# From coroutine stages with hand-set due times to one list schedule over single instructions, in a two-layer transformer kernel

## The chip, the cores and the metric

The kernel runs on one core of one Trainium2 chip. The metric is the device time of one execution in microseconds (us). A core has five engines, each with its own in-order instruction stream: PE (the matrix engine; its weight loads are listed apart as PEld), DVE (vector), ACT (scalar, which evaluates functions), POOL and SP (which here only issues DMAs). PE writes only to PSUM, which DVE and ACT read; the rest of the data lies in SBUF.

## The reference

2048 tokens of width 128 (four sequences of 512, here called blocks 0 to 3) pass through four residual sublayers. In short:

```
x = x + attention(layernorm(x))    # causal, 16 heads of 8
x = x + moe(layernorm(x))          # 8 experts of width 512, gelu, top 2,
                                   # a capacity per expert counted over all tokens in order
x = x + gated_recurrence_and_ffn(layernorm(x))
    # q, k, v, gate: 128 -> 1024; state = decay*state + k*v along the sequence;
    # out = gate*q*state -> Wo; then layernorm, 128 -> 512 -> 128 with gelu
x = x + ternary_ffn(layernorm(x))  # silu(x W1)*(x W2), two 512 -> 512 layers with gelu, 512 -> 128
```

The blocks are independent of each other but for one thing: the running count of tokens per expert goes from block to block in the routing.

## The kernel before, in words

Each block goes through eight stages: **project** (layernorm, transposes, q and k for groups of four heads, v), **maxima** (a first pass over the scores for the row maxima: PE writes `s`, DVE reduces it to `mx`), **weights** (scores again less the maxima, ACT takes `exp` into `ex`, POOL cuts the triangle, PE multiplies by v into the one PSUM bank `po`), **output** with **route** (layernorm, logits, a string of small DVE operations, then 8 indirect DMAs that put each token into rows of `xgd`), **experts** (read the rows back as `xg`, two layers for each of 8 experts, results to `ygd`, 8 indirect DMAs `got` back), **recurrence** (8 chunks of 128 channels: four projections `pp`, a scan on DVE, then `por`), **feed** (the gelu layer) and **ternary** (four layers, each operand split into a high and a low part `hh`, `hl`). A ninth stage, **setup**, loads constants and writes the rounded ternary weights (`round_weights`, lines 975 to 989: DMA to `stage`, POOL rounds and subtracts, DVE reduces to `odd`, which tells whether the general path at the end of the kernel is needed; it is not taken with these inputs).

PSUM holds three single banks that all dense work shares (`bank()`, tag `pt`), two pairs of banks for scores (`s`) and one for `po`. Expert weights `ew` have three buffers, recurrence weights `rw` three.

PE, DVE, ACT and SP run their instructions in the order in which the program issues them. That order is made while the kernel is built. Every stage is a Python coroutine that issues a piece and yields. `play` (line 305) picks the next piece: it keeps a modelled clock of each engine (`Clock`, line 50, with the cost of each operation in `cost`, line 123), looks at which stages could go on at PE's present time, and takes the one whose due time `start` is lowest; the due time then grows by the PE work of the piece times a `stretch`. Start and stretch are set by hand per stage (lines 1096 to 1105), at 140 us a block:

```python
    at = 140.0 * b
    stages[f"project{b}"] = Stage(-4e3, 1.0, "pt", project(b))
    stages[f"maxima{b}"] = Stage(max(at - 145.0, 0.0), 3.5, "s", maxima(b))
    stages[f"weights{b}"] = Stage(-5e3 if b else 1.0, 1.0, "s", weights(b))
    stages[f"experts{b}"] = Stage(at, 1.3, "pt", experts(b))
    stages[f"recurrence{b}"] = Stage(at + 60.0, 1.0, "pt", recurrence(b))
    stages[f"feed{b}"] = Stage(at + 158.0, 1.4, "pt", chain(feed(b), ternary(b)))
```

A stage also yields names of other stages that it waits for. Some are data dependences. Others are order alone: `weights{b}` waits for `experts{b-1}` and `feed{b-2}` (lines 442 to 448), `experts{b}` for `experts{b-1}`, `recurrence{b}` for `recurrence{b-1}`, `feed{b}` for `output{b+1}` and `feed{b-1}`. Within a piece the instructions stand as the stage writes them, and each operation has one engine, written in the code: for instance the copies of transposes on ACT, the copy of `po` on DVE, the triangle on POOL.

Of the kernel before, what the change touches and what calls it, by code (L numbers as in the profile page):

```python
# [10 lines left out]
F32 = mybir.dt.float32  # L11
# [9 lines left out]
P = 128  # L21
D = 128
# [21 lines left out]
def block_kernel(ctx: ExitStack, tc: tile.TileContext, i: dict, out: bass.AP):  # L44
# [4 lines left out]

    class Clock:  # L50

        def __init__(self):
            self.now = dict.fromkeys(("PE", "DVE", "ACT", "POOL", "SP"), 0.0)
            self.used = {}
            self.turns = {}
            self.end = self.work = 0.0
            self.table = None

        def span(self, ap):
            if ap.tensor.name not in self.used:
                self.used[ap.tensor.name] = []
                tag = getattr(ap.tensor, "tag", None)
                if tag is not None:
                    self.turns.setdefault(tag, []).append(ap.tensor)
            if ap.space == DRAM:
                lo = ap.offset
                hi = lo + sum(s * (n - 1) for s, n in ap.ap)
            else:  # L70
                lo = ap.offset % ap.ap[0][0]
                hi = lo + sum(s * (n - 1) for s, n in ap.ap[1:])
            return lo, hi

        def bufs(self, tensor):
            return tensor.bufs or tensor.tag_meta.bufs

        def over(self, tensor):
            return max((x[4] for x in self.used.get(tensor.name, ())), default=0.0)

        def slot(self, tag):

            t = self.turns.get(tag, ())
            return self.over(t[-self.bufs(t[-1])]) if t and len(t) >= self.bufs(t[-1]) else 0.0

        def ready(self, engine, ap, write):
            lo, hi = self.span(ap)
            at = 0.0
            for x in self.used[ap.tensor.name]:
                if x[3] != engine and x[0] <= hi and lo <= x[1] and (write or x[2]):  # L90
                    at = max(at, x[4])
            tag = getattr(ap.tensor, "tag", None)
            if tag is not None and not self.used[ap.tensor.name]:
                t = self.turns[tag]
                n = self.bufs(ap.tensor)
                if len(t) > n:
                    at = max(at, self.over(t[-1 - n]))
            return at

        def note(self, engine, op, args, kw):  # L100
            out = kw["out"] if "out" in kw else args[0]
            ins = [x for x in (*args, *kw.values()) if isinstance(x, bass.AP) and x is not out]
            ins += [x.ap for x in (*args, *kw.values()) if isinstance(x, bass.IndirectOffsetOnAxis)]
            took, after = self.cost(engine, op, out, ins, kw, args)

            who = "PUT" if op.startswith("indirect") and out.space == DRAM else "DMA" if "dma" in op else engine
            at = max([self.ready(who if who == "PUT" else engine, out, True)] + [self.ready(engine, x, False) for x in ins])
            begin = max(self.now[engine], at)
            self.now[engine] = begin + took
            end = begin + took + after  # L110
            for x, write in [(out, True)] + [(x, False) for x in ins]:
                lo, hi = self.span(x)
                keep = self.used[x.tensor.name]
                if write:
                    keep[:] = [k for k in keep if not (lo <= k[0] and k[1] <= hi)]
                keep.append((lo, hi, write, who, end))
                if len(keep) > 64:
                    keep[:] = [k for k in keep if k[4] > self.now["PE"] - 300.0]
            self.end = max(self.end, end)
            if engine == "PE":  # L120
                self.work += took

        def cost(self, engine, op, out, ins, kw, args):
            n = out.free_size()
            if "dma" in op:
                size = 4.0 * math.prod(out.shape) if engine != "POOL" else 4.0 * P * P
                return {"SP": 0.45, "ACT": 0.1, "POOL": 1.0}[engine], 1.9 + size / 2.0e5
            if engine == "PE":
                if op == "transpose":
                    return 0.11, 0.2  # L130
                w, x = kw["lhsT"], kw["rhs"]
                n = x.free_size()
                if w.partition_size() == HP:
                    return max(0.03, n * 1.7e-4), 0.2
                if w.free_size() < HP and n > HP and w.free_size() == DK + 1:
                    return max(0.11, n * 6.5e-4), 0.2
                if w.dtype == F32:
                    return max(0.22, n * 1.68e-3), 0.2
                return max(0.06, n * 4.5e-4), 0.2
            if engine == "ACT":  # L140
                load = 0.0
                f = args[2] if op == "activation" else None
                if f in (AF.Exp, AF.Gelu) and f != self.table:
                    self.table, load = f, 1.3
                return load + (0.22 + 9.1e-4 * n if n <= S else 0.42 + 4.9e-4 * n), 0.1
            if engine == "DVE":
                if op == "tensor_reduce":
                    n = ins[0].free_size()
                    return 0.06 + 1.08e-3 * n, 0.1
                if op == "tensor_tensor_scan":  # L150
                    return 1.25, 0.1
                if n <= 64:
                    return 0.12, 0.1
                if op in ("tensor_copy", "memset") and all(x.space != PSUM for x in ins):
                    return 0.1 + 6.5e-4 * n, 0.1
                return 0.1 + 1.2e-3 * n, 0.1
            if op == "memset":
                return 0.1 + 9.0e-4 * n, 0.1
            return {"affine_select": 0.6, "iota": 0.6}.get(op, 0.25 + 2.1e-3 * n if n > 64 else 1.0), 0.1

    clock = Clock()

    class Engine:
# [3 lines left out]
        def __getattr__(self, op):  # L167
            def issue(*args, **kw):
                ins = getattr(self.engine, op)(*args, **kw)  # L169
                clock.note(self.name, op, args, kw)  # L170
                return ins

            return issue

    class nc:
        vector, scalar, gpsimd, sync, tensor = (
            Engine(n, e) for n, e in (
                ("DVE", tc.nc.vector), ("ACT", tc.nc.scalar), ("POOL", tc.nc.gpsimd), ("SP", tc.nc.sync),
                ("PE", tc.nc.tensor),
            )  # L180
        )
        values_load = tc.nc.values_load

# [13 lines left out]
    small = ctx.enter_context(tc.tile_pool(name="small", bufs=4))  # L197
    scr = ctx.enter_context(tc.tile_pool(name="scr", bufs=2, space=DRAM))
    work = ctx.enter_context(ExitStack())
    att = work.enter_context(tc.tile_pool(name="att", bufs=1))  # L200
    rt = work.enter_context(tc.tile_pool(name="rt", bufs=1))
    ps_s = work.enter_context(tc.tile_pool(name="ps_s", bufs=2, space=PSUM))
    ps_o = work.enter_context(tc.tile_pool(name="ps_o", bufs=1, space=PSUM))
    pools(work, "", y=1, moe=1, ew=3, rec=2, rw=3, ff=8, p_d=1)

    work.enter_context(tc.manual_schedule(engines=IN_ORDER))
    mm = nc.tensor.matmul
# [20 lines left out]
    xs = state.tile([P, NT, D], F32, name="xs")  # L228
    x_v = i["x"].rearrange("(n p) d -> p n d", p=P)
# [9 lines left out]
    def moments(src):  # L239

        st = small.tile([P, TB, 6], F32, tag="ln_st", name="ln_st")
        mv = small.tile([P, TB, 2], F32, tag="ln_mv", name="ln_mv")
        for t in range(TB):
            nc.vector.bn_stats(st[:, t, :], src[:, t, :])
        for t in range(TB):
            nc.vector.bn_aggr(mv[:, t, :], st[:, t, :])
        return mv
# [9 lines left out]
    def layernorm(src, dst):  # L257

        mv = moments(src)
        rs = small.tile([P, 2, TB], F32, tag="ln_rs", name="ln_rs")  # L260
        nc.vector.tensor_scalar(rs[:, 0, :], mv[:, :, 1], EPS, None, ALU.add)
        nc.gpsimd.tensor_tensor(rs[:, 0, :], rs[:, 0, :], mhalf[:, 0, :], ALU.pow)
        yield WAIT
        scaled(src, mv, rs[:, 0, :], dst)
        yield WAIT

    def flip(src):

        pt = bank("pt", shape=(P, TB, P))
        for t in range(TB):  # L270
            transpose(pt[:, t, :], src[:, t, :])
        return pt
# [3 lines left out]

    def y_tile(who):
        return At.y.tile([P, TB, D], F32, tag="y" + who, name="y", bufs=2 if who == "a" else 1)

    def turned(y, who, gain=None, shift=None):  # L280
# [6 lines left out]
        return yT  # L287

    GO, WAIT = 0, 1

    def run(stage):
# [908 lines left out]
```

## Time and profile before

| | us |
|---|---|
| median of 5 runs | 835.54 (834.39 to 841.73) |
| the profiled execution: its time, its span | 834.4, 832.6 |
| mean granted PE clock in it | 0.868 of full speed |
| busy PE, PEld, DVE, ACT, POOL | 677.6, 382.0, 465.3, 279.1, 182.4 |
| DMA | 46.37 MB, mean 56 GB/s |

The span runs from the first to the last instruction; the profiled execution's time is 1.8 us longer. Where the stages lie in it, by the start of the first and last instruction of each kind, in us from the span's start:

| block | `pqk` matmuls | `mx` reductions | `exp` | expert `ph` | `pp` matmuls | first `pa` of ternary to `res` |
|---|---|---|---|---|---|---|
| 0 | 9.9 to 19.2 | 21.7 to 98.1 | 52.3 to 111.3 | 169.6 to 194.1 | 234.2 to 295.3 | 361.4 to 394.3 |
| 1 | 121.8 to 131.6 | 138.1 to 193.7 | 200.5 to 238.3 | 311.3 to 352.5 | 404.0 to 479.4 | 545.6 to 578.5 |
| 2 | 257.1 to 267.1 | 298.1 to 341.1 | 395.3 to 424.9 | 495.6 to 536.7 | 588.1 to 646.4 | 701.3 to 735.6 |
| 3 | 445.2 to 461.4 | 482.3 to 525.3 | 579.5 to 609.0 | 663.4 to 692.4 | 735.4 to 767.3 | 795.2 to 826.1 |

In the views, nearly all instructions carry line 169, the helper through which all are issued, so they are told apart by tile names. An entry `ex<-s` is the instruction that writes `ex` from `s`. Matmul ends are modelled, and matmuls overlap, so a busy PE may still be slow: the granted clock has to be read with it.

### The profile page before, as it was taken

To read this page: it belongs to the slowest core of one execution; us is meant where nothing else is said; L and a number is where in the kernel's file an instruction comes from. 1 tells how busy PE (TensorE), PEld (TensorE's weight loads), DVE (VectorE), ACT (ScalarE), POOL (GpSimd) and SP (SyncE) were. 2 spreads that over 40 slices of the span, in tenths; PEclk is the share of its full clock that TensorE was granted. 3 is DMA by queue.
4 is the path that set the end of the run, shared out by engine and by line. 5 is a ranking of instruction groups with operands and counts; after the bars stand their busy time and mean duration, and the time that the engine had idled before them with its cause. 6 is when DMAs were issued, how large, how long until landed. Compare 5 with 4: busy or idle time off the path is not lost.

```text
span 832.6 us, 9464 instructions
## 1 busy us (share of the span) xinstructions
PE 677.6 (81%) x3302; PEld 382.0 (46%) x3302; DVE 465.3 (56%) x1082; ACT 279.1 (34%) x460; POOL 182.4 (22%) x249
## 2 busy tenths in 40 slices
PE   5168977896797889969995989978998597899676
PEld 2024334394343347636442447645443385544244
DVE  5256338822357777476367667374368414778263
ACT  3022332054453213413752222414642162233221
POOL 1064220302520400042320400042321403200110
PEclk9655698588799989989998889969999798999888
DMA  6521000244001123320110113320010252021000
GB/s 150 178 66 38 3 13 1 89 122 144 13 17 35 52 62 99 95 72 1 34 36 21 58 50 106 95 60 25 14 38 33 83 146 60 10 60 29 1 0 17
DMA packets 73623, 46.37 MB, mean 56 GB/s; under 512 B 9696, under 2 KB 66528, under 8 KB 73568
## 3 DMA queue, kind: packets, MB, share of 16 engines
q1 hardware_dynamic: 70944, 41.23, 17.2%
q0 software_dynamic: 2048, 4.20, 1.7%
q8 instruction: 28, 0.46, 0.2%
q10 hardware_dynamic: 576, 0.26, 0.1%
q14 instruction: 27, 0.22, 0.1%
HBM read 35.71 MB, written 9.96 MB: 55 GB/s over the span
## 4 chain that ended last, share of the span: by engine, by line
PE 52%; DVE 25%; issue 10%; ACT 4%; SPq 3%; DMA 3%; POOL 2%; ACTq 0%; DVEq 0%; POOLq 0%
PE s L169 12%; PE ph L169 9%; PE pp L169 7%; PE po L169 6%; PE py L169 4%; PE por L169 4%; DVE mx L169 4%; PE pt L169 3%; SPq L169 3%; DVE a L169 3%; PE pqk L169 2%; DVE st L169 2%; DVE oc L169 2%; DVE hl L169 2%; DVE hh L169 2%
## 5 line engine op out<-in xcount | busy, mean ns | idle before, releaser
L169 PE MATMUL pp<-yT,rw 128*128 128x512 f32 x256 | 125.0, 621 | 4.6 <-ACT g L169 1.1
L169 DVE TENSOR_REDUCE mx<-s 128x2 f32<-128x1024 f32 (+3 forms) x128 | 100.2, 819 | 26.8 <-PE s L169 25.8
L169 ACT ACTIVATE ex<-s 128x768 f32<-128x768 f32 (+1 forms) x96 | 79.8, 880 | 63.3 <-PE s L169 60.8
L169 PE MATMUL s<-ks,qs 32*128 32x128 f32 (+3 forms) x256 | 62.5, 485 | 36.6 <-DVE mx L169 35.7
L169 PEld LDWEIGHTS pp<-yT,rw 128*128 128x128 f32 x256 | 44.8, 193 | 61.1 <-issue 32.9
L169 POOL TENSOR_TENSOR ln_rs<-ln_rs,mhalf 128x4 f32<-128x4 f32 (+1 forms) x20 | 23.7, 1187 | 208.2 <-DVE ln_rs L169 207.9
L169 POOL TENSOR_SCALAR_AFFINE_SELECT ex<-ex 128x256 f32<-128x256 f32 (+1 forms) x96 | 48.8, 512 | 92.3 <-ACT ex L169 91.3
L169 PE MATMUL po<-ex,vs 128*9 128x128 f32 (+3 forms) x512 | 53.7, 506 | 9.4 <-issue 9.1
L169 PE MATMUL ph<-hh,r_h_w 128*128 128x512 f32 x128 | 53.4, 417 | 7.3 <-DVE hh L169 6.9
L169 ACT ACTIVATE hT<-ph,w_mb 128x192 f32<-128x192 f32 x128 | 45.2, 419 | 37.0 <-PE ph L169 36.5
L169 PEld LDWEIGHTS s<-ks,qs 32*128 32x128 f32 x256 | 28.2, 217 | 63.6 <-DVE mx L169 41.8
L169 DVE TENSOR_SCALAR xT<-py,w_mb 128x192 f32<-128x192 f32 x32 | 13.4, 418 | 75.8 <-PE py L169 69.4
L169 POOL DMA_INDIRECT xgd<-y,rt_at x32 | 34.5, 1077 | 96.5 <-DVE rt_at L169 87.9
L169 PE MATMUL ph<-hl,r_h_w 128*128 128x512 f32 x128 | 53.4, 417 | 2.3 <-DVE hl L169 2.3
L169 PE MATMUL ph<-xT,ew 128*128 128x192 f32 x256 | 51.9, 340 | 0.7 <-ACT hT L169 0.5
L169 DVE COPY oT<-po 128x512 f32<-128x512 f32 x16 | 11.0, 690 | 74.0 <-PE po L169 74.0
L169 PE MATMUL pqk<-yT,wide 128*128 128x512 f32 x64 | 39.8, 763 | 15.4 <-DVE wide L169 11.4
L169 PE MATMUL s<-qs,ks 32*128 32x128 f32 (+3 forms) x256 | 41.9, 429 | 7.8 <-ACT ex L169 6.7
L169 PE MATMUL py<-hT,ew 128*128 128x192 f32 x256 | 46.8, 328 | 0.0
L169 PEld LDWEIGHTS ph<-xT,ew 128*128 128x128 f32 x256 | 42.8, 197 | 3.6 <-issue 1.7
L169 POOL DMA_INDIRECT got<-ygd,rt_at x32 | 31.2, 975 | 58.6 <-ACT ex L169 47.8
L169 PEld LDWEIGHTS s<-qs,ks 32*128 32x128 f32 x256 | 21.9, 213 | 48.2 <-ACT ex L169 35.2
(187 smaller groups left out, 1098.9 us busy)
## 6 DMA issues: line engine op xcount, KB each, us to landing
ew<-in_E_dram SPq DMA_DIRECT2D x64, 256.0 KB
xg<-xgd SPq DMA_DIRECT2D x4, 768.0 KB
ygd<-og SPq DMA_DIRECT2D x16, 192.0 KB
stage<-in_h_w_dram SPq DMA_DIRECT2D x8, 256.0 KB
rw<-in_Wk_dram SPq DMA_DIRECT2D x32, 64.0 KB
rw<-in_Wv_dram SPq DMA_DIRECT2D x32, 64.0 KB
rw<-in_Wg_dram SPq DMA_DIRECT2D x32, 64.0 KB
rw<-in_Wq_dram SPq DMA_DIRECT2D x32, 64.0 KB
```

Source lines behind the costliest of these rows:

```text
L169: ins = getattr(self.engine, op)(*args, **kw)
```

## The change

The stages become plain functions that are run once, block by block, without issuing anything: each call of an engine is noted as a task with its tiles (`Plan.note`). Tasks depend on earlier tasks that wrote or read the same data. Then `Plan.order` simulates the five engines: at each step it takes the engine whose next task can begin earliest, and among its tasks that could begin within 0.1 us of that the one with the longest path of work behind it. `Plan.issue` emits the real instructions in that order. The due times, `play`, and the waits between stages are gone. Two kinds of order between blocks are kept as `plan.hold`: a recurrence after the one of the block before, from its transposed input on, and feed with ternary after the ternary of the block before.

A tile is no longer given a buffer where the program writes it down; it gets a slot when its first task is ordered, in the order of its own stage for the small shared kinds. Some operations may go to either of two engines, whichever would end first in the model: copies out of PSUM (ACT or DVE), an expert's last bias (DVE or ACT), the high and low parts in ternary (DVE or POOL), the triangle (POOL as one instruction, or DVE as two). The model also has a PE clock of half or full speed, a price for changing ACT's function table, matmuls of 32 rows beside each other, and DMAs that land one after the other. In block 0 the maxima use single `pt` banks instead of the pairs. The layernorm tiles of recurrence, feed and ternary share one buffer (`yc`). The count of buffers and the arithmetic are otherwise as before; every matmul is there in the same number.

The core of the diff:

```diff
-    def play(live):
-        through = {}
-        while live:
...
-            now = max(clock.now["PE"], min(free.values()))
-            soon = min((t for n, t in free.items() if live[n].start < 0), default=1e9)
...
-            n = min((n for n, t in free.items() if t <= now), key=lambda n: live[n].start)
...
+        def order(self):
+            for task in reversed(self.tasks):
+                way = next(iter(task.ways.values()))
+                after = sum(way[2]) if isinstance(way[2], tuple) else way[2]
+                task.weight = way[1] + after + max((t.weight for t in task.before), default=0.0)
...
+            while len(done) < len(self.tasks):
+                best = None
+                for e in ENGINES:
+                    starts = []
+                    for task in can[e]:
+                        t = self.begin(task, e)
+                        if t is None:
+                            continue
+                        if len(task.ways) > 1:
+                            end = t + task.ways[e][1]
+                            others = [
+                                x + task.ways[o][1] for o in task.ways if o != e and (x := self.begin(task, o)) is not None
+                            ]
+                            if others and min(others) < end - 0.01:
+                                continue
+                        starts.append((t, task))
...
+                first, engine, starts = best
+                near = [(t, x) for t, x in starts if t <= first + NEAR]
...
+                t, task = max(near, key=lambda x: x[1].weight)
...
+        def begin(self, task, engine):
+            t = self.now[engine]
+            if task.table is not None and task.table != self.table:
+                t += TABLE
+            for e, r in task.ready.items():
+                if e != engine and r > t:
+                    t = r
+            for lent in task.lents:
+                if lent.slot is None:
+                    if not lent.slots.free or lent.queue[0] is not lent:
+                        return None
+                    t = max(t, min(lent.slots.until[k] for k in lent.slots.free))
+            return t
...
+    TABLE, NEAR = 1.3, 0.1
...
         if "dma" in op:
             size = 4.0 * math.prod(out.shape) if engine != "POOL" else 4.0 * P * P
-            return {"SP": 0.45, "ACT": 0.1, "POOL": 1.0}[engine], 1.9 + size / 2.0e5
+            return {"SP": 0.45, "ACT": 0.1, "POOL": 1.0}[engine], (1.6, size / 2.5e5)
...
+    def copy(dst, src):
+        with one_task():
+            nc.scalar.copy(dst, src)
+            if plan.recording:
+                nc.vector.tensor_copy(dst, src)
...
     def weights(b):
-        if b > 0:
-            yield f"experts{b - 1}"
-        if b > 1:
-            yield f"feed{b - 2}"
...
-            nc.gpsimd.affine_select(
...
+            with one_task():
+                nc.gpsimd.affine_select(
...
+                for j in range(2):
+                    nc.vector.scalar_tensor_tensor(
+                        e[:, j], e[:, j], 2.0, upper.unsqueeze(1).to_broadcast([P, len(part), P]), ALU.min, ALU.mult,
+                    )
...
     def halves(h, c):
-            nc.vector.tensor_copy(hi, h)
-            eng = nc.gpsimd if c == 1 else nc.vector
-            eng.tensor_tensor(lo, h, hi, ALU.subtract)
+            with one_task():
+                for x in (nc.vector, nc.gpsimd):
+                    x.tensor_copy(hi, h)
+            with one_task():
+                for x in (nc.vector, nc.gpsimd):
+                    x.tensor_tensor(lo, h, hi, ALU.subtract)
...
     def recurrence(b):
-        yield f"experts{b}"
-        yield f"recurrence{b - 1}" if b > 0 else "scales"
...
         if b > 0:
-            yield f"begun{b - 1}"
+            plan.hold = [lasts[b - 1]]
...
+    plan.stage = "setup"
+    setup()
     for b in range(NB):
-        at = 140.0 * b
-        stages[f"project{b}"] = Stage(-4e3, 1.0, "pt", project(b))
...
-    play(stages)
+        for stage in (project, maxima, weights, output, experts, recurrence, feed, ternary):
+            plan.stage = f"{stage.__name__}{b}"
+            stage(b)
+    plan.issue()
```

829 lines of the change are left out of this document (465 added, 364 removed).

## The prediction

> **What bounds the kernel now.** I read the page first: busy times, then the slices, then the chain.
>
> ```profile
> PE 677.6 (81%) x3302; PEld 382.0 (46%) x3302; DVE 465.3 (56%) x1082; ACT 279.1 (34%) x460; POOL 182.4 (22%) x249
> PE   5168977896797889969995989978998597899676
> PEclk9655698588799989989998889969999798999888
> PE 52%; DVE 25%; issue 10%; ACT 4%; SPq 3%; DMA 3%; POOL 2%; ACTq 0%; DVEq 0%; POOLq 0%
> ```
>
> PE is the fullest engine, and over half of the chain that ended last is PE. But a slice with a 7 or 8 for PE often has a 5 to 8 for the granted clock: PE loses time by idling, and again by being slowed. So I cut the span at the stages' borders and asked for busy time and clock in each stretch. The columns are the stretch, then busy us of PE, PEld, DVE, ACT and POOL with instruction counts, then the granted PE clock, the DMA share and GB/s.
>
> ```profile
> 0.00:45.00 45.00, 15.84 (x52) 7.38 (x52) 18.01 (x51) 6.77 (x11) 6.82 (x30) 0.79 0.56 153
> 45.00:120.00 75.00, 62.00 (x407) 28.38 (x407) 36.75 (x78) 23.11 (x29) 30.71 (x50) 0.67 0.10 29
> 120.00:169.00 49.00, 38.63 (x161) 20.13 (x162) 39.34 (x101) 6.47 (x12) 9.09 (x9) 0.65 0.14 43
> 169.00:311.00 142.00, 117.07 (x633) 65.70 (x631) 72.01 (x177) 55.81 (x96) 32.84 (x44) 0.89 0.23 65
> 311.00:496.00 185.00, 161.82 (x829) 92.39 (x830) 113.82 (x263) 70.21 (x116) 40.24 (x50) 0.93 0.18 52
> 496.00:680.00 184.00, 161.12 (x849) 98.54 (x849) 102.62 (x248) 73.96 (x131) 40.87 (x49) 0.92 0.22 65
> 680.00:735.00 55.00, 45.44 (x173) 31.03 (x172) 28.29 (x71) 17.67 (x32) 14.66 (x13) 0.91 0.15 39
> 735.00:832.60 97.60, 75.69 (x208) 38.42 (x208) 54.44 (x98) 25.11 (x37) 7.17 (x6) 0.91 0.08 23
> ```
>
> Busy PE times the clock of its stretch is roughly what the same matmuls would need at full clock: 12.5 + 41.5 + 25.1 + 104.2 + 150.5 + 148.2 + 41.4 + 68.9 = 592.3 us. The span is 832.6, so 240.3 us are lost: 155.0 idle (832.6 - 677.6) and 85.3 to the half clock (677.6 - 592.3). DVE, the next engine, has 465.3. Hence the floor for any order of these instructions is far below today's time, and the question is how much of the 240 an order can get back.
>
> The losses have places. From 311 to 680 the kernel is periodic (the chunks of recurrence 1 and 2, the expert runs and the exps of the table lie 184 us apart); there PE does (150.5 + 148.2) / 369 = 81% of full-clock work. Around it: 120 to 169 is maxima 1 and route 0 with nothing else, at 51% (25.1 / 49); 735 to the end is recurrence, feed and ternary of block 3 in series, at 71% (68.9 / 97.6); 0 to 120 is block 0's attention with setup beside it, at 45% (54.0 / 120). Three more views show typical stalls: groups of waits (us in total, times, longest), the timeline of DVE and PE, and one group of ACT.
>
> ```profile
> PE s L169 <- DVE mx L169: 36.3, 21, 19.1
> 38.16 0.17 DVE L169 TENSOR_SCALAR dec<-dec 128x8 f32<-128x8 f32 x1 [13.17 <-ACT dec L169]
> 139.35 0.69 PE L169 MATMUL s<-ks,qs 32*128 32x384 f32 x2 [4.99 <-DVE mx L169]
> L169 ACT ACT_TABLE_LOAD x8 | 10.3, 1283 | 3.3 <-issue 2.9 <-PE s L169 0.3
> 416.30:437.10 20.80, 20.67 (x142) 9.64 (x140) 12.85 (x36) 11.00 (x16) 6.04 (x10) 1.00 0.13 36
> ```
>
> The 19.1 us: PE waits for a maximum on DVE, which stands 13.17 us behind a setup instruction whose DMA comes late. The 4.99 us: DVE works through route's small operations in written order while PE waits for a reduction queued behind them. Both are order, not data. The last line, a stretch where weights, recurrence and ternary work lie beside each other, shows 99% of full-clock work: PE can be filled when three stages are open at once.
>
> **The change, step by step.** *Waits between stages go.* `weights{b}` no longer waits for `experts{b-1}` and `feed{b-2}`: attention 1 (exps from 200.5 today) can follow attention 0 (last exp 111.3) at once, and 2 and 3 behind it. Dense work of earlier blocks fills PE between the score matmuls, which today run at half clock when alone (0.67 and 0.65 above). What still binds is data: `qs`, `ks`, `vs` and `po` are single, so attentions pipeline by head group; recurrences and the feed/ternary pairs stay in series; block 3's recurrence, feed and ternary remain the end of the longest path.
>
> First 120 us: nothing but setup can lie beside block 0 there, in either order. The 19.1 us stall can go. It can also come back: the order rests on DMAs at 250 GB/s, the page's best slice moved 178, and whatever DVE has queued behind `stage` or `dec` waits as today. Bounds 0 and -19; I take -8, nearer to no gain, since the same late DMAs feed the same queue. 112 us.
>
> 120 to 735 (615 us, need 592.3 - 54.0 - 68.9 = 469.4 us, now 76%): the floor is the 99% slice, but no order holds that for 500 us, so 97% is the best end: 469.4 / 0.97 = 484. The other end is today's periodic 81%: 580. I take 88%, a little under the middle, because three shared PSUM banks stay and every evicting engine is in order: 469.4 / 0.88 = 533 us. So -82.
>
> Last 97.6 us: recurrence 3, feed 3, ternary 3 in series, need 68.9. Leftovers of block 2 may fall into it, and its own gaps may shrink. Bounds 0 and -19 (68.9 / 0.88 = 78); I take -8: 90 us.
>
> *Evictions on either engine.* The 16 copies of `po` (11.0 us on DVE) and the 8 `xT` copies (4.7 us on ACT) go where there is room; DVE's 465.3 over some 735 us is 63%, so this is cover for the 88%, not a term of its own. On POOL a low part takes 1296 ns against 693 on DVE; if the planner sent all 48 there, POOL would gain about 36 x 1.3 = 47 us on its 182.4: still the emptiest, priced at nothing while ternary is not last, and at 0.6 us for each that is.
>
> *Exp and gelu mixed.* Today 8 table loads cost 10.3 us of ACT. With exps beside experts and ternary there may be more: none at best; at worst all 96 exps stand alone between gelus, 192 x 1.28 = 246 us. The planner adds 1.3 us to a start that changes the table, so it changes only when nothing else can start sooner; I take 40 loads, 32 x 1.28 = 41 us more on an engine that is 34% busy. Covered by ACT's idle time; uncovered, it is up to 41 us on the attention chain, well inside the 484 to 580.
>
> [...] In the trace a table load is followed at once: load at 394.05 for 1.28 us, next exp at 395.34. [...]
>
> *More waiting queues.* SP issues loads in the modelled order, and a load that waits for its buffer holds those behind it. Today, DVE waits 5.4 us in all for `ew` and PE 0.8 for `rw`. A planned 256 KB load is worth 1.05 us of transfer at 250 GB/s; at the slice's 178 it is 1.47. For the 64 `ew` loads that is 27 us if none were ahead; with three buffers most is hidden. In the 88%.
>
> Sum: 112 + 533 + 90 = 735 for the span; 1.8 us outside it (834.4 against 832.6) and 1.1 from that execution to the median (835.54) give 738. All good ends: 101 + 484 + 78 + 3 = 666. All bad ends: 120 + 580 + 98 + 3 = 801.
>
> **The rivals.** *Little of it arrives:* PE is held by the three banks and by single tiles, not by the order, and the middle stays near 81%. For it: DVE is 62% busy in 311 to 496 and evictions queue there. Against it: the 99% slice has the same banks. Time 801, spread 775 to 831.
>
> *Slower: the order is planned on wrong times.* PE, DVE, ACT and SP can't pass an instruction that waits, and single instructions of many stages now alternate, so each late landing stops all stages at once; today a piece keeps to one stage. Place: the 64 users of fetched weights (32 experts, 32 chunks of recurrence). Price: 64 times the mean wait; at 2 us each, 128 on top of 738 makes 866. It decides from 1.5 us, where 64 x 1.5 = 96 eats the whole gain. For it: the 13.17 us above is such a stall, caused by one DMA; the planner's bandwidth is 1.4 times the best slice. Against it: outside the start, today's waits for these loads are 6 us in all, and mean durations in the rows (621 ns with overlap for a matmul, 690 for a 512-wide eviction, 1225 for a scan) are near the planner's costs.
>
> **How the numbers follow.** About 0.5% is what can be told from no change here. Forecast (675 to 775): 0.55. Below it: 0.05. Little arrives (775 to 831): 0.15. Within 0.5%: 0.03. Slower: 0.22, of which 0.13 lies above 850. So faster 0.75, same 0.03, slower 0.22. The range 675 to 850 leaves out 0.05 and 0.13. The forecast's own range is 675 to 775.
>
> **What would show it.** Right: exps of block 1 start before 150 and those of block 3 end before 480; PE does 85 to 92% of full-clock work from 120 to 650, with the clock above 0.95 there; PE idle falls from 155 to some 90 us; 20 to 80 table loads. First step wrong: DVE still stands over 10 us in the first 60. Last step wrong: more than 100 us from recurrence 3's first projection to the end. The slower rival: waits of PE or DVE on `ew` or `rw` DMAs, or PE idle above 155. The forecast as a whole fails if PE idle and half-clock loss together stay above 200 us.

## The result: no change, and the profile after

The kernel after takes 835.17 us (median of 44 runs, 829.87 to 836.59) against 835.39 for the kernel before (86 runs). The ratio is 0.9992, interval 0.9984 to 0.9999. Forecast was 738 us. So the forecast gain of 97 us is absent, although the order of nearly every instruction is new. The profiled execution has a span of 829.5 us and a time of 831.3, which is 3.9 under the median; so the 3 us between the two spans mean nothing.

The page of the kernel after: busy times, the slices of PE and of its clock, the chain that ended last.

```profile
PE 680.6 (82%) x3302; PEld 384.1 (46%) x3302; DVE 491.8 (59%) x1222; ACT 305.0 (37%) x478; POOL 166.7 (20%) x204
PE   6489888778959896998689987996899598599585
PEclk9558856589888997999799998999899699799888
PE 27%; DVE 9%; issue 6%; POOL 4%; ACT 2%; DMA 0%; another core or an unknown queue 0%; DVEq 0%; ACTq 0%; POOLq 0%
```

PE is as full as before, and its clock row still has the 5s and 6s of the first fifth. The chain can't be set beside the one before: its shares add up to 48%, since it is followed back only to 425.05 us, and within that half PE has 27 of the 48. The same cuts as in the prediction (stretch, busy us of PE, PEld, DVE, ACT, POOL with counts, PE clock, DMA share, GB/s):

```profile
0.00:45.00 45.00, 25.18 (x92) 12.71 (x92) 25.68 (x94) 8.34 (x12) 9.28 (x34) 0.77 0.66 183
45.00:120.00 75.00, 66.10 (x418) 34.23 (x416) 54.52 (x144) 24.60 (x34) 27.09 (x38) 0.73 0.11 33
120.00:169.00 49.00, 38.75 (x186) 19.41 (x186) 31.41 (x86) 10.23 (x15) 9.22 (x10) 0.57 0.07 23
169.00:311.00 142.00, 122.18 (x642) 66.20 (x642) 86.27 (x198) 54.71 (x91) 15.79 (x20) 0.91 0.21 58
311.00:496.00 185.00, 158.86 (x831) 90.27 (x829) 117.76 (x287) 81.43 (x124) 34.54 (x36) 0.93 0.18 51
496.00:680.00 184.00, 153.85 (x759) 93.34 (x758) 94.84 (x263) 87.37 (x140) 43.46 (x45) 0.91 0.24 69
680.00:735.00 55.00, 43.71 (x178) 30.19 (x177) 31.16 (x67) 15.56 (x32) 14.35 (x13) 0.91 0.18 50
735.00:829.50 94.50, 72.01 (x206) 37.71 (x205) 50.12 (x87) 22.78 (x34) 12.93 (x11) 0.89 0.06 17
```

Busy PE times the mean clock of each stretch sums to 592.6 us, the need of before (592.3) within rounding. So 236.9 us of the span are lost: 148.9 idle and 88.0 to the half clock, where before had 155.0 and 85.3. The stretch from 120 to 169 does only 22.1 us of full-clock work, less than before (25.1).

Equal cuts in time compare unequal work, so I cut again where PE has done the same share of its full-clock work, now by the trace's record of the clock itself (the first 14 us, ahead of its first entry, are counted at half clock): 8.9%, reached at 120 us before and at 97.9 after, and 88.3%, at 735 and 731.4. First the kernel before, then the kernel after:

```profile
0.00:120.00 120.00, 77.84 (x459) 35.76 (x459) 54.76 (x128) 29.88 (x40) 37.53 (x79) 0.72 0.27 76
120.00:735.00 615.00, 524.08 (x2637) 307.79 (x2638) 356.08 (x858) 224.12 (x384) 137.70 (x164) 0.89 0.20 57
735.00:832.60 97.60, 75.69 (x208) 38.42 (x208) 54.44 (x98) 25.11 (x37) 7.17 (x6) 0.91 0.08 23
```

```profile
0.00:97.90 97.90, 72.86 (x410) 37.47 (x414) 65.91 (x202) 27.91 (x38) 34.04 (x68) 0.76 0.38 106
97.90:731.40 633.50, 532.18 (x2686) 307.63 (x2682) 373.07 (x932) 253.22 (x405) 118.31 (x125) 0.88 0.19 54
731.40:829.50 98.10, 75.61 (x215) 38.97 (x213) 52.77 (x91) 23.89 (x36) 14.32 (x12) 0.90 0.07 19
```

The start is 22 us shorter. The middle, for the same work, is 18 us longer (633.5 against 615.0) where the forecast had 533. The tail is equal. So the 22 us won at the start were given back in the middle, and the 82 that the forecast had for the middle didn't come.

What the middle waits for shows in PE's waits (us in total, times, longest; of the whole span, of the first line 17.4 us lie in the middle) of the kernel after:

```profile
PE pt L428 <- DVE yc L428: 24.8, 4, 9.1
PE s L428 <- ACT ex L428: 14.4, 10, 5.2
PE po L428 <- POOL ex L428: 12.6, 2, 6.4
PE s L428 <- DVE mx L428: 12.1, 14, 2.7
```

The third line is new (0.2 us before): PE waits twice for a triangle cut on POOL. The timelines of POOL, then of PE, around the first of the two, in the kernel after:

```profile
389.21 1.03 POOL L428 DMA_INDIRECT xg<-ygd,rt_at  x1 [0.17 <-issue]
...
398.55 0.94 POOL L428 DMA_INDIRECT xg<-ygd,rt_at  x1 [0.30 <-issue]
399.50 0.65 POOL L428 TENSOR_SCALAR_AFFINE_SELECT ex<-ex 128x512 f32<-128x512 f32 x1
```

```profile
400.20 1.47 PE L428 MATMUL po<-ex,vs 128*9 128x256 f32 x16 [6.23 <-POOL ex L428]
```

Eight gathers (indirect DMAs that read rows back) run first, then the triangle, then PE goes on: it has stood 6.23 us with ternary work of another block queued behind the stopped matmul. This isn't the planned order. In `Plan.order` both triangles that PE waits for stand between the fifth and the sixth of their eight gathers. But the kernel has the order of issue kept for PE, DVE, ACT and SP alone (line 48), not for POOL, and in the program that ran each stands behind the eighth. No run has POOL's order kept too.

### The profile page after: what moved, and what is told of

Read it like the earlier page. It is cut to its first block, busy times and chain, and to the rows that moved or that the text cites. A ratio compares the mean times of both kernels' runs of the same rounds, so it can differ in the third digit from the quotient of the medians.

```text
span 829.5 us, 9646 instructions
## 1 busy us (share of the span) xinstructions
PE 680.6 (82%) x3302; PEld 384.1 (46%) x3302; DVE 491.8 (59%) x1222; ACT 305.0 (37%) x478; POOL 166.7 (20%) x204
## 5 line engine op out<-in xcount | busy, mean ns | idle before, releaser
L428 PE MATMUL pt<-yTr,rw 128*128 128x512 f32 x256 | 127.9, 623 | 2.4 <-DVE oc L428 1.5
L428 DVE TENSOR_REDUCE mx<-s 128x2 f32<-128x512 f32 (+3 forms) x96 | 74.1, 815 | 3.1 <-PE s L428 2.9
L428 PEld LDWEIGHTS pt<-yTr,rw 128*128 128x128 f32 x256 | 45.2, 193 | 56.4 <-issue 19.6
L428 PE MATMUL po<-ex,vs 128*9 128x128 f32 (+3 forms) x512 | 50.2, 484 | 15.6 <-POOL ex L428 12.6
L428 PE MATMUL pt<-xT,ew 128*128 128x192 f32 x256 | 53.4, 348 | 6.7 <-ACT hT L428 5.5
L428 PE MATMUL pt<-hh,r_h_w 128*128 128x512 f32 x128 | 52.9, 470 | 5.1 <-ACT h L428 2.1
L428 PE MATMUL pt<-hT,ew 128*128 128x192 f32 x256 | 53.7, 349 | 3.0 <-ACT hT L428 1.7
L428 PE MATMUL s<-qs,ks 32*128 32x128 f32 (+3 forms) x256 | 41.2, 421 | 15.9 <-ACT ex L428 14.4
L428 PE MATMUL pt<-yTp,ex 128*128 128x512 f32 x64 | 45.4, 816 | 8.6 <-DVE qs L428 2.7
L428 ACT ACTIVATE hT<-pt,w_mb 128x192 f32<-128x192 f32 x128 | 44.1, 421 | 21.4 <-PE pt L428 21.2
L428 PEld LDWEIGHTS pt<-hT,ew 128*128 128x128 f32 x256 | 43.6, 198 | 11.1 <-ACT hT L428 5.3
L428 PE MATMUL pt<-hl,r_h_w 128*128 128x512 f32 x128 | 48.7, 447 | 0.0
L428 ACT ACT_TABLE_LOAD x32 | 41.1, 1283 | 19.1 <-PE pt L428 11.4
L428 POOL TENSOR_TENSOR hl<-h,hh 128x512 fp32r<-128x512 f32 x16 | 22.8, 1423 | 114.8 <-DVE hh L428 114.6
```

What stands on the lines that cost most here:

```text
L428: task.ins = getattr(getattr(nc, NAMES[task.engine]), op)(*map(self.real, args), **{k: self.real(v) for k, v in kw.items()})
```

## The experiments

Two theories stood at first. **A:** the order is planned on wrong times (the second rival of the prediction, with other places than the fetched weights). **B:** structure binds whatever the order: three dense banks, single tiles, chains within a block. All kernels start from the kernel after unless said otherwise; "middle" is again the time between the same shares of PE's work, "idle" is PE's in it, "half" the part of PE's busy time there that the half clock cost (from the trace's record of the clock).

| kernel | median us | ratio to before (interval) | middle | idle | half |
|---|---|---|---|---|---|
| before | | | 615.0 | 91.0 | 51.6 |
| after | 835.17 | 0.9992 (0.9984 to 0.9999) | 633.5 | 101.3 | 57.4 |
| e1_dec | 834.14 | 0.9977 (0.9952 to 1.0002) | 635.6 | 100.7 | 62.1 |
| e2_costs | 819.97 | 0.9806 (0.9770 to 0.9842) | 615.1 | 89.2 | 52.2 |
| e3_costs_dve_triangle | 809.58 | 0.9699 (0.9672 to 0.9725) | 606.5 | 87.3 | 41.1 |
| e4_fixed_engines | 817.72 | 0.9798 (0.9771 to 0.9826) | 616.3 | 89.7 | 57.1 |
| e5_one_number | 828.49 | 0.9911 (0.9880 to 0.9943) | 629.6 | 95.8 | 61.9 |
| e6_costs_copies_halves | 790.23 | 0.9461 (0.9423 to 0.9500) | 581.1 | 71.0 | 42.4 |
| e8_halves_fixed | 813.38 | 0.9733 (0.9703 to 0.9762) | 607.4 | 79.0 | 56.5 |
| e10_halves_fixed_again | 815.42 | 0.9726 (0.9683 to 0.9768) | 610.4 | 82.3 | 55.8 |
| e11_costs_copies_halves_again | 813.98 | 0.9725 (0.9693 to 0.9758) | 612.9 | 90.8 | 47.6 |
| e12_costs_halves | 818.33 | 0.9793 (0.9750 to 0.9837) | 614.4 | 87.2 | 53.5 |
| e13_triangle_alone | 818.24 | 0.9814 (0.9758 to 0.9869) | 616.9 | 91.0 | 46.8 |
| e14_gpsimd_bare | 821.35 | 0.9823 (0.9779 to 0.9866) | 620.1 | 89.5 | 55.1 |
| e15_five_banks_one_pair | 820.86 | 0.9846 (0.9775 to 0.9917) | 614.4 | 78.2 | 58.2 |
| e17_triangle_again | 810.30 | 0.9711 (0.9688 to 0.9735) | 611.7 | 81.3 | 54.3 |
| e18_all_together | 809.14 | 0.9704 (0.9674 to 0.9734) | 605.1 | 84.6 | 42.1 |

**The late DMA at the start.** The kernel after stalls as the prediction feared: ACT, in order, stands until `dec` lands, and a maximum on DVE with it (timelines of ACT and DVE, kernel after).

```profile
31.49 0.21 ACT L428 ACTIVATE dec<-dec 128x8 f32<-128x8 f32 x1 [15.93 <-DMA dec<-in_decay_logit_dram]
```

```profile
31.73 0.17 DVE L428 TENSOR_SCALAR dec<-dec 128x8 f32<-128x8 f32 x1 [9.90 <-ACT dec L428]
```

e1 tells the order about it.

```
-            return {"SP": 0.45, ...}[engine], (1.6, size / 2.5e5)
+            name = "" if isinstance(out, View) else out.tensor.name
+            return {"SP": 0.45, ...}[engine], (14.6 if name.startswith("dec") else 1.6, size / 2.5e5)
```

> Only the planner's idea of one load is changed: the decay logits land 13 us later in its model, as they do in the trace of after (issued at 18.4, user at 31.5). Theory A (the order is planned on wrong times, and every late landing stops in-order engines): the stall of 9.9 us on DVE and 11 us on PE near 32 us goes, and since nothing behind catches up, the time falls by 9 to 12 us, to 823 to 826. Theory B (single tiles, three PSUM banks and the serial chains bind, whatever the order): the slack behind absorbs it, within 3 us of 835.

834.14 us: nothing, within 1 us of the kernel after. The wait moved on to the next late loads (DVE now stands 5.54 us until `w_bg` lands). The start was not what was lost; its 22 us had been won in spite of it.

**Measured times in the cost function.** From the profile after: indirect DMAs on POOL 1.27 us start to start (planned 1.0), small DVE operations 0.21 (planned 0.12), `bn_aggr` 0.09, the wide power 1.75.

```
-            return {"SP": 0.45, "ACT": 0.1, "POOL": 1.0}[engine], (1.6, size / 2.5e5)
+            name = "" if isinstance(out, View) else out.tensor.name
+            slow = 13.0 if name.startswith("dec") else 0.0
+            return {"SP": 0.45, "ACT": 0.1, "POOL": 1.27}[engine], (1.6 + slow, size / 2.5e5)
-                return 0.06 + 1.08e-3 * ins[0].free_size(), 0.1
+                return max(0.21, 0.06 + 1.08e-3 * ins[0].free_size()), 0.1
+            if op == "bn_aggr":
+                return 0.09, 0.1
-                return 0.12, 0.1
+                return 0.21, 0.1
-        ... 0.25 + 2.1e-3 * n if n > 64 else 1.0), 0.1
+        ... 0.25 + 2.1e-3 * n if n > 64 else 1.0 if n <= 4 else 1.75), 0.1
```

> The planner's costs are set to what the trace of after shows: indirect DMAs on POOL 1.27 us apart instead of 1.0, small DVE operations 0.21 instead of 0.12, batch-norm aggregation 0.09, the wide power on POOL 1.75, and the late decay load. Nothing else. Theory A: the stalls at the four routes and four gathers shrink as well as the one at the start; 30 to 55 us less, 780 to 805. Theory B: 815 to 832.

819.97: some 15 us of the 97, within B's band and not A's. e3 adds the triangle on DVE only (the `affine_select` is dropped from the alternatives).

> As the kernel with corrected costs, and the triangle of the exponentials is cut on DVE alone, so that it can't stand behind eight indirect DMAs on POOL. Theory A: the two waits of PE on the triangle (6.2 us each in after, around 400 and 581) go, but DVE has some 30 us more work: 775 to 805, within 10 of the kernel with corrected costs. Theory B: slower than that kernel by 5 to 15, since DVE is nearly full beside maxima and recurrence.

809.58, 10 us less again; B, which had it slower, was wrong on the triangle, and A's band (775 to 805) missed it too.

**The choice of engine.** e4 keeps the costs of the change and gives every operation the engine it had before: the copies of banks, the second expert layer's eviction, the halves `hh` and `hl` of ternary, the triangle.

```
-            nc.scalar.copy(dst, src)
-            if plan.recording:
-                nc.vector.tensor_copy(dst, src)
+        nc.scalar.copy(dst, src)
-            copy(oT, po)
+            nc.vector.tensor_copy(oT, po)
-                for x in (nc.vector, nc.gpsimd):
-                    x.tensor_copy(hi, h)
+                nc.vector.tensor_copy(hi, h)
-                    x.tensor_tensor(lo, h, hi, ALU.subtract)
+                (nc.gpsimd if c == 1 else nc.vector).tensor_tensor(lo, h, hi, ALU.subtract)
...
```

> After without the choice of engine: each operation on the one engine it had before the change. Theory A: the choice is worth little, 825 to 840. Theory B: evictions hold the banks, so losing the choice costs 10 to 25 us: 845 to 860.

817.72. B expected a loss and A next to nothing; neither had it that the freedom to choose costs, here 17 us.

**How much is luck of the order?** A control: one cost moves by 0.6%.

```
-                return max(0.22, n * 1.68e-3), 0.2
+                return max(0.22, n * 1.69e-3), 0.2
```

> One number of the cost function is moved by 0.6% (a full-precision matmul from 1.68 to 1.69 ns per column); nothing else. It is a control: it reorders many instructions on VectorE and ScalarE but means nothing. If the order of the kernel after is good or bad for a reason, this stays within 8 us of 835; if the order's time is largely luck, it may land anywhere from 815 to 855, and then the 15 to 25 us that the earlier edits gained count for less.

828.49, 7 us less for nothing. Differences of this size prove nothing here, so three of the later edits were repeated with this number changed. e6 joins measured costs with fixed copies and halves:

> The measured costs of e2_costs, and the copies out of PSUM and the halves of the ternary layers fixed to the engines that they had before the change; the triangle still on either. If the two causes (times that are wrong, engines chosen by these times) are separate, the gains add: 835 - 16 - (most of 17) = 803 to 812. If the wrong engine was chosen only because its time was wrong, the costs have already put that right and it stays at 815 to 823.

790.23, the fastest kernel of the study, 5.4% under before. Its repetition decides whether that has a cause:

> e6_costs_copies_halves with the same meaningless 0.6% on top. If the 790 has causes, this gives 783 to 800; if 790 was one lucky order, it falls back among the other kernels with measured costs, 808 to 822.

813.98. It hasn't: 24 us between two kernels that differ by a number without meaning. 790 is a kernel that can be used, but no reason is shown for it. The middle of e6:

```profile
104.40:685.50 581.10, 510.13 (x2641) 299.56 (x2639) 372.70 (x935) 242.83 (x400) 109.47 (x111) 0.91 0.21 59
```

Even this order does 510.13 x 0.91 / 581.1 = 80% of full-clock work in the middle.

**Which freedom cost it?** First the halves alone fixed, twice (e10 with the changed number):

> The kernel after with the halves of the ternary layers alone fixed as before the change (first half on VectorE, the difference on VectorE but for one in four on GpSimd). If the free choice of this pair is what cost the 17 us of e4_fixed_engines, it lands at 815 to 824; if the copies or the triangle did, at 830 to 838.

> e8_halves_fixed with the meaningless 0.6% of e5_one_number on top. If the gain of the fixed halves is real and not the luck of one order, it is again 15 to 28 us under the 828 to 835 of the kernels with free halves: 805 to 817. If it was luck, it lies anywhere between 805 and 840, most likely at 820 to 835.

813.38 and 815.42: real, but not yet a cause, for in these orders the triangles, still free, no longer fell behind gathers either. e13 leaves halves and copies free and takes only the triangle off POOL; e17 repeats it in the other order.

```
-                nc.gpsimd.affine_select(
-                    out=e, in_=e, compare_op=ALU.is_ge, fill=0.0, base=0,
-                    pattern=[[0, 2], [0, len(part)], [1, P]], channel_multiplier=-1,
-                )
```

> The kernel after with the triangle on VectorE only; halves and copies free, costs as in the change. The profile after has two triangles that run behind eight gathers on GpSimd and hold TensorE 6.2 and 6.4 us. If these are what the free choice costs, the time is 12 to 18 us under 835: 817 to 823, like the kernels with fixed halves. If the halves themselves cost it, 829 to 838.

> e13_triangle_alone with the meaningless 0.6% of e5_one_number on top. If triangles behind the gathers are what the free choice costs, it is again at 810 to 823, some 8 to 18 us under e5 (828). If e13 was luck, 824 to 838.

818.24 against 835.17, and 810.30 against 828.49 of e5: 17 and 18 us (15 and 17 by the ratios), with halves free both times. So fixing the halves isn't needed for the gain. e5 has the wait for the triangle as well (the line is of its PE waits), while PE waited for `ex` of ACT only 4.4 us there instead of 14.4.

```profile
PE po L428 <- POOL ex L428: 16.0, 3, 6.2
```

That makes e5 against e17 the cleaner pair: between them the wait for POOL goes from 16.0 us to nothing, and that for ACT stays small (4.4 and 6.4). From the kernel after to e13 both fall, POOL's from 12.6 to nothing and ACT's from 14.4 to 4.0. Over all list-scheduled kernels with three single banks the wait for POOL's triangle parts the slow from the fast: 12.6, 12.7 and 16.0 us in the kernel after, e1 and e5 (828 to 835 us), at most 9.3 in the others (790 to 821). It isn't POOL itself that costs: e4 cuts all 96 triangles there, with 3.3 us of such waits, and takes 817.72. What differs is their place behind the gathers. One clean pair, beside a luck of 7 to 24 us, supports this strongly but doesn't settle the 17 us.

The two waits of the kernel after are 12.6 us; about 6 us more come with them, as the clock shows. Windows of the kernel after, the last around the stop at 400:

```profile
105.81:126.29 20.48, 18.28 (x66) 8.67 (x64) 14.14 (x31) 2.34 (x4) 1.01 (x1) 0.50 0.04 14
255.99:320.85 64.86, 56.00 (x251) 23.79 (x249) 57.17 (x126) 18.19 (x26) 7.81 (x9) 1.00 0.13 39
395.94:406.18 10.24, 5.97 (x27) 4.07 (x28) 5.90 (x23) 0.59 (x1) 5.16 (x5) 0.50 0.10 26
```

After the stop PE's work runs at half clock until 406.18: 5.97 us of it, of which half, 3.0 us, is lost. The second stop has the same, 5.90 us busy at half clock from 576.85 to 587.09. The second window, mostly recurrence of block 0, is 86% busy at full clock throughout. The first will matter below.

**Do the parts add?** e12 has measured costs and fixed halves; e14 takes both halves and the triangle off POOL at the costs of the change; e18 joins costs, halves, copies and triangle.

> The measured costs of e2_costs and the halves alone fixed, the copies out of PSUM free again. If halves and costs carry the gain of e6 and the copies none, 786 to 800. If the copies matter (a copy that ScalarE and VectorE share is the hand-over of almost every bank), 803 to 815.

> The kernel after with both halves and the triangle on VectorE only: GpSimd keeps the puts, the gathers, the powers, one addition per block and the setup. If the work on GpSimd behind the puts and gathers is the only loss, 803 to 815, not above e8_halves_fixed (813). If VectorE is by now close to being the bound (some 530 us busy), it lies above 820.

> The measured costs of e2_costs, halves and copies fixed, and the triangle on VectorE only. If the parts add, 780 to 800. If they all take away the same few stalls and the rest is held by banks and the half clock, 805 to 820 like each of them alone.

818.33, 821.35, 809.14. They don't add. All eleven kernels with measured costs, fixed halves or no triangle on POOL, the banks and the work as they were (e2, e3, e4, e8, e10 to e14, e17, e18) lie from 809 to 821 and need 605 to 620 us for the middle; only e6 stands apart. Nearly all are rid of the same few stops: PE's wait for POOL's triangle is 0 to 3.3 us in them, but for 9.3 in e2.

**What holds the middle then?** First, does TensorE's work set the time? e7 shortens 176 ternary matmuls, so its output is not the full product.

```
-                mm(ps, lhsT=w, rhs=x, start=start and n == 0, stop=stop and n == 1)
+                mm(ps[:, : S if n == 0 else 64], lhsT=w, rhs=x[:, : S if n == 0 else 64],
+                   start=start and n == 0, stop=stop and n == 1)
```

> The kernel after, but the matmuls on the low half of the ternary layers take 64 of 512 columns: 176 matmuls of about 0.23 us become short, some 30 us of TensorE work at full clock less, with the same instructions, waits and buffers. If TensorE's work sets the time (the forecast's rule, need over 0.88), it falls by 30 to 36 us to 799 to 806. If chains and single tiles set it, TensorE only waits more and it falls by less than 12, to 823 to 835.

800.16 us, ratio 0.9594 (0.9551 to 0.9638): 35 less. Its PE work at full clock is 577.2 us against 598.1, both from the clock record, so 20.9 less; but orders with all the work differ in this number too, from 589 in e6 to 604 in e13. Its waits for POOL's triangle are 2.3 us, so it belongs beside the eleven orders above, and is 9 to 21 us under them. Work taken from PE gives time, then; that it does so one for one isn't shown, and e6, with all the work, is faster still.

Second, the banks, on top of e8: five single banks and one pair for scores (e15), two single banks and two pairs (e16).

```
-        return At.p_d.tile(list(shape), F32, tag="pt", name=name, bufs=3)
+        return At.p_d.tile(list(shape), F32, tag="pt", name=name, bufs=5 if isinstance(At.p_d, Memory) else 3)
-        return At.p_s.tile([P, 2, S], F32, tag="s", name="s")
+        return At.p_s.tile([P, 2, S], F32, tag="s", name="s", bufs=1)
```

These are e15's lines; e16 has `bufs=2` in the first of them and keeps the two pairs.

> e8_halves_fixed with the banks cut otherwise: five instead of three single banks for dense products, one instead of two pairs for the attention scores. If the dense banks hold TensorE, the stages without attention get shorter, and the sum is 785 to 805; if the score pairs are what the exps live on, their stretches grow and it is 820 to 860; near 813 if neither binds.

> e8_halves_fixed with two instead of three single banks for dense products. If the banks hold TensorE, this is far slower, above 880; if chains set the time, under 840.

820.86 and 986.65 (ratio 1.1784, 1.1731 to 1.1837). One bank less costs 173 us; two more, bought with a pair, give nothing. PE's waits in e15 show where they went, against 5.5 us in 11 times for the second line in e8:

```profile
PE s L428 <- DVE mx L428: 23.5, 23, 2.7
PE s L428 <- ACT ex L428: 16.3, 38, 1.2
```

Three single banks, two pairs and the one of `po` make eight; no run here uses more, so more dense banks without fewer pairs were not tried.

Third, the half clock. In all kernels with the full work and three single banks it takes 41 to 62 us of the middle, whatever the order, and 18 to 31 of the part ahead of it. The first window above is the reason for e9: PE is 89% busy with attention's 32-row products and the dense ends of it, no wait of PE in it is over 1.46 us, and the clock is 0.50 from end to end. e9 puts a dense matmul ahead of each pair's products in the exps of blocks 0 and 1, and in the same way in the maxima of block 1, 72 in all, on e6:

```
             ps = pair()
+            if b < 2:
+                mm(ps[:, 0, :], lhsT=spread[:, 0, :], rhs=spread.rearrange("p g q -> p (g q)"), start=True, stop=True)
```

> On top of e6_costs_copies_halves: before the 32-row products of each pair of banks in the exps of blocks 0 and 1 and the maxima of block 1, one dense matmul of 128 rows and 512 columns that means nothing (72 of them, about 0.23 us each, 16.6 us at full clock; the products that follow overwrite its result). In e6 these stages hold 50 of the 81 us that are lost to the half clock. If the clock stays halved there because the products keep too few rows of the array at work, dense work between them brings it back: the half-clock loss falls by 20 us or more and the time stays at 775 to 793 in spite of the added work. If it does not, the added work shows: 803 to 815.

817.75, ratio 0.9796 (0.9737 to 0.9855). The half clock's share of the middle is 44.5 us (42.4 in e6, 47.6 in e11), so the filler didn't bring the clock back. How far the 28 us over e6 are its work and how far e6's luck can't be told from one run.

All twenty traces together tell more. The record of the clock moves in steps of 3.41 us, so I cut PE's time into such pieces and took for each the share in which a matmul of 128 rows was running. Take only pieces in which PE was busy for 90% or more. At full clock, half clock followed 23 of 27 with a share under 0.4, and 2 of 2138 with a share of 0.5 or more. At half clock, full clock followed 3 of 101 with a share under 0.5, 125 of 275 between 0.5 and 0.9, and 231 of 237 at 0.9 or more. So in these traces a PE that was busy with products of 32 rows went with the half clock even where nothing waited. In the half-clock pieces of the first 260 us this share is 0.49 on average in e6 and 0.54 in e9: the filler hardly moved it, so e9 doesn't speak against few rows as the cause. This is a count over traces; no run changed the rows alone, so the cause is likely but not shown.

## Why the prediction failed

**The step that failed** is "I take 88%" for the middle: 469.4 / 0.88 = 533 us. Measured, the kernel after does 532.18 x 0.88 / 633.5 = 74%, so 633.5 us: 100 us off, the whole error and a little more. Three things were wrong in it, the first by far the largest. What sets the idle time that remains in every order stays open.

- *The floor.* 99% came from one slice of 21 us. It held for three stages of the right kinds, not for the middle's mix. Idle and half clock were taken as one loss of which an order recovers half, and dense work between the score products was to bring the clock above 0.95; it is 0.88 in the middle, and the half clock costs 57.4 us there against 51.6 before. The runs part them: over all orders with the full work and three banks, idle in the middle goes from 71 to 101 us, and the half clock stays at 41 to 62. 533 us allow 64 us for both. With a half clock of 50 that leaves 14 us of idle, and no order came below 71.
- *The bad end.* 801 us, today's periodic 81%, was not the worst for this order. The kernel before had 76% over this whole middle, so even the bad end took 35 us of gain for granted, and stops that a new order brings were left out. The triangles behind gathers, with the half clock that follows, cost some 17 us by e13 and e17.
- *"This is cover for the 88%, not a term of its own."* Free engines were priced at nothing, but the freedom of the triangle is those 17 us, as far as e13 and e17 show it.

The planner's own times don't foretell it either. Added up, the model in `Plan.order` ends at 757 us for the kernel after, 19 above the forecast and 78 under the measurement. Over all orders with the full work and three single banks it ends at 752 to 786 and doesn't rank them: e17 and e5 end at 752 and measure 810 and 828, e18 ends at 786 and measures 809.

**The other terms.** First 120 us: forecast -8, measured -22 (120.0 to 97.9 for the same work), although the stall did come back with 11.08 us of PE waiting for DVE; the sign "DVE over 10 us" stood at 9.90. What shrank is block 0's own attention: PE's idle time in the start went from 42.2 to 25.0 us, and the exps of block 0 are over at 99.9 us, where the last began at 111.3 before. Last 97.6 us: forecast -8, measured +0.5. Together -21.6 against -16: near in sum, but by luck, as one term is nearly three times its forecast and the other nothing. Table loads: 40 forecast, 32 measured, 41.1 us of ACT; no run changed them alone, so that they are covered isn't shown. One more pair of lines from ACT's timeline of the kernel after:

```profile
334.44 1.28 ACT L428 ACT_TABLE_LOAD   x1
335.73 1.51 ACT L428 ACTIVATE ex<-s 128x768 f32<-128x768 f32 x2
```

The exp starts 0.01 us after the load's end, as the one at 395.34 did before.

**The signs.** From 120 to 650 PE was to do 85 to 92% of full-clock work at a clock over 0.95; the middle has 74% at 0.88. Exps of block 1 start at 159.5 (before 200.5; 150 was asked), the last of block 3 starts at 573.5 (480 was asked). PE idle 148.9, not 90. Idle and half clock stay at 236.9, above the 200 at which the forecast as a whole was to fail. Recurrence 3's first projection to the end is 109.7 us, over the 100 of the sign, but at equal work the tail is unchanged: leftovers of other blocks lie in it.

**The rivals.** "Little of it arrives" (801) had the direction: the order doesn't free PE, and e16 shows how near the banks are. Its level, 81%, no kernel with this work reaches; the lucky e6 has 80%. "Planned on wrong times" was named with the wrong place: there is no wait of PE or DVE for `ew` or `rw` after. That an order on wrong times costs fits e2, where mending the times gave 15 us; this edit alone was not repeated. Neither alone is the result.

In the kernel after, the half clock came with a stop and without one. Around the stop from 394 to 400 the clock had halved at 395.94, when PE had stood 2 us, and is full again at 406.18, after 3.41 us that PE filled. The window from 105.81 to 126.29 has no such stop: 20.48 us at half clock with PE 89% busy. It fits the count above: of the six pieces of that window none has a matmul of 128 rows running for 0.9 of it (0.61 to 0.85).

## What to carry to other kernels

Before pricing a new order, split the lost time of the bound engine into what waits cost and what its clock costs, and ask for each whether any order in the trace has less of it; a best slice is no floor for a mix of stages. If operations that the bound engine waits for share an engine with a run of indirect DMAs, see that they don't end up behind it, and check whether the program that runs has that engine's planned order at all. And where a list schedule makes the order, move one number by half a per cent first: here this alone moved the time by 7 and by 24 us, so a single kernel that is 1 or 2% faster shows nothing until it is repeated in another order.

## What was not expected of the hardware

- `hl` takes longer on average after: on POOL 1423 ns against 1296 before, on DVE 789 against 693, with the same shape. The medians hardly move (1300 and 692): three on DVE take 1752 to 1777 ns, each while POOL works on another `hl`, and POOL's longest, 2241 ns, lies beside a scan and two other operations of DVE. In the kernel before no `hl` takes over 1304 ns. Three others on DVE that overlap with one on POOL keep 684 to 689; what parts the two kinds was not tried.
- `dec`, two loads of 2.0 KB each whose values are picked one by one (elements of 4 bytes), lands 7.7 and 12.3 us after its issue in the kernel after (median 10.0); the 256 KB of an `ew` land in 2.8 (median).
- Twice in the kernel after, exps stop while the eight puts of a block are issued. ACT's timeline of it, the second:

```profile
505.29 1.51 ACT L428 ACTIVATE ex<-s 128x768 f32<-128x768 f32 x2 [5.84 <-issue]
```

PE had issued the products that this exp reads by 499.90, but its semaphore events pause from 499.07 to 505.21, and six that were due come within 0.3 us when the last put has landed (505.19). The other pause is from 316.64 to 322.28. e1 has both too; e5, e8, e6 and e13 have none, so the step from the kernel after to e13 holds this loss as well. Why it comes was not found, and stays open.
